# Two five-block feature buffers and filler block products in a four-layer graph kernel

## The chip, the cores and the metric

The kernel runs on one core of a Trainium2 chip, in 32-bit floats. The metric is the device time of one execution in microseconds (us). A profile of one further execution gives the span from its first to its last instruction and what each engine did: PE (TensorE, matrix products), DVE (VectorE), ACT (ScalarE), POOL (GpSimd), and SP (SyncE), which here only issues DMA transfers. PE's results land in PSUM, eight banks of 128 x 512 values.

## The reference

The input is 128 batches of 128 nodes x 512 features and one 128 x 128 matrix `adj`. Four layers follow each other, each added to its input and normalised over the features:

```python
x = _layernorm(x + _L0(x, adj, w0, bias0))        # adj @ x @ w0 + bias
x = _layernorm(x + _L1(x, w1, a, beta, adj))      # graph attention, elu
x = _layernorm(x + _L2(x, adj, adj, b2))          # reduces to relu(max_n(adj @ x) + b2)
x = _layernorm(x + _L3(x, w_qkv, w_proj, ..., adj))  # 8-head masked attention
```

Layer 3 makes q, k and v (512 x 1536 weights), scores of 8 heads of width 64, masks where `adj` is 0, a softmax, the product with v, a projection, and a normalisation with gamma and beta of its own, before the outer one.

## The kernel before, in words

**A batch** is one chain of steps (`batch`, L884). Layer 0: a product with `adj` (L281 for the first 12 batches, "direct"; later L300, whose result is transposed on DVE and regrouped by a trip through DRAM, x_d), a product with w0 (L273, four matmuls of 512 columns), then addition and normalisation. Layer 1: two logits per node (L920), an attention matrix made for two batches at a time (`attention1`, L577, which goes through DRAM twice, s_d and e_d), a product with it (L281), a product with w1 (L273), elu, normalisation. Layer 2: one product (L952), a maximum, normalisation. Then the features are transposed (L967) and sent to DRAM (`features`, L865), and the rows themselves are kept in DRAM too (`spill`, L870, `fetch`, L877).

**Groups.** Batches of one group share the work on q, k and v. There are 2 groups of two (FIRST), 28 of four (G) and 6 of two (PAIRS): 36. `gather` (L642) brings a group's features back, turned, as four blocks B11, B21, B12, B22, and POOL makes three further ones by four subtractions (L663): T3, T1 (in the place of B12), T2 and T4. The tile xT has seven blocks, and there is one such tile. `section` (L668), once each for q, k and v, makes the product with the weights as a 2 x 2 block product in Winograd's form: seven products instead of eight, each of 4 matmuls at L686 (256 columns in a group of four; 128 in a pair for q and k), with partial results copied by ACT (L721, L793) and added by DVE (L735). Three sections of seven products read xT, after which it is free.

**Attention** of layer 3: `tiled` and `score` (L803, L828) compute a group's scores (L834). Per batch DVE adds the mask (L984) and takes the maximum (L991), ACT takes eight exponentials (L1005), DVE multiplies by the reciprocal sums (L1012) and transposes (L1015); the probabilities go to DRAM (p_d, L1020) and come back regrouped (L1024), into the tile that held q and k. `attend` (L840) multiplies them with v (L855), two batches at a time, and `usual` (L1052) does the projection (L273), the sums and the output. q and k of a whole group lie in one tile qkT (two such tiles); v lies in one tile for each half of a group (four).

**What sets the order.** Nothing is scheduled by hand. `Plan` (L63) runs all chains against each other before the program is written. A step asks for an engine with its planned duration, and perhaps a buffer (`use`), and says with `late` how long after it its result is usable; a request is granted at the earliest time at which its engine, its inputs and its buffer are free, ties going by urgency and then by rank, the lower first. The granted order is the order of the instructions on each engine. The engines then run these in order, with semaphores where a result is needed, so the plan's durations decide only the order. A batch's rank is its number; block products have the group's first number plus SECTION (2) plus a part. The planned times of transfers are the `late` values of SP's steps. Buffers are counted in BUFS.

Small tiles (statistics, 128 x 1 values and the like) come from a pool that rotates through 12 buffers for each name.

Of the kernel before, what the change touches and what calls it, by code (L numbers as in the profile page):

```python
# [18 lines left out]
G = 4  # L19
FIRST = 2  # L20
PAIRS = 6
SOON = (0, 4, 0, 4, 10, 0)
# [3 lines left out]
RUN = 6  # L26
SECTION = 2
PACE = 0
# [11 lines left out]
    "ps": 8,  # L40
    "x": 12, "xr": 2, "yT": 4, "z": 1, "e": 1, "et": 1, "eT": 3, "t": 5, "xT": 1, "v": 4,
    "qkT": 2, "pt": 1,
}
LAST, AHEAD = 14, 4
DIRECT = 12
LATER = -0.1
LANDED = 4.0
# [3 lines left out]

B11, B21, B12, B22, T3, T2, T4 = range(7)
T1 = B12
BLOCKS = 7
A11, A12, A22, S1, S2, S3, S4 = range(7)
# [97 lines left out]
def gnn_stack_kernel(  # L153
# [22 lines left out]
    work = ctx.enter_context(tc.tile_pool(name="work", bufs=1))  # L176
    small = ctx.enter_context(tc.tile_pool(name="small", bufs=12))
    ps = ctx.enter_context(tc.tile_pool(name="ps", bufs=1, space=PSUM))
# [213 lines left out]
    def loads():  # L392
        yield use("SP", 0.4)
        nc.sync.dma_start(adj_sb, adj)
        landing(adj_in, P // 4)
        yield from load(0, "ACT", nc.scalar)
        w0_slot.append((yield use("SP", 0.0, "qkT")))
        w0_nat.append(
            buf(w0_slot[0], G, 2 * K, P).rearrange("p b c n -> p (b c n)")[:, : K * D].rearrange(
                "p (k o) -> p k o", k=K  # L400
            )
        )
        for k in range(K):
            yield use("SP", 0.4)
            nc.sync.dma_start(w0_nat[0][:, k, :], w0[k * P : (k + 1) * P])
            landing(w0_chunk[k], P)
        yield from load(1)
        yield use("SP", 0.4)
        nc.sync.dma_start(bias0_sb, rows(bias0, D))
        landing(bias0_in, P)  # L410
        for i in range(2, 4):
            yield from load(i)
        slot = yield use("SP", 1.0, "pt")
        matrix(w1_sb, w1)
        a_sb = buf(slot, H, P).rearrange("p (s k) f -> p s (k f)", s=2)
        nc.sync.dma_start(a_sb, rows(a, 2 * D).rearrange("p (s f) -> p s f", s=2))
        landing(w1_in, (K + 2) * P)
        plan.start(logit_rows(a_sb, slot), 0)
        for i in range(4, 8):
            yield from load(i)  # L420
        yield use("SP", 2.0)
        permuted(w0_sb, w0)
        landing(w0_in, K * P)
        yield use("SP", 1.0)
        nc.sync.dma_start(beta1_sb, rows(beta1, 1))
        nc.sync.dma_start(
            b2_sb, bass.AP(tensor=b2.tensor, offset=b2.offset, ap=[[1, P], [1, 1]])
        )
        landing(scalars_in, 2 * P)
        for i in range(8, 12):  # L430
            yield from load(i)
        yield use("SP", 2.5)
        permuted(wqkv_sb, w_qkv)
        matrix(wproj_sb, w_proj)
        for dst, src in ((bproj_sb, b_proj), (gamma_sb, gamma), (beta3_sb, beta3)):
            nc.sync.dma_start(dst, rows(src, D))
        landing(w3_in, (4 * K + 3) * P)
        plan.start(weight_sums(), 0)
        for i in range(12, NB):
            yield from load(i)  # L440
# [81 lines left out]
    class Group:  # L522


        def __init__(self, first, size):
            self.first, self.size, self.half = first, size, size // 2
            self.s = small.tile([P, G, 2], F32, name="s")
            self.logits = [Event(2) for _ in range(size // 2)]
            self.attention = [Event() for _ in range(size // 2)]
            self.summed, self.qk = Event(), Event(8)  # L530
            self.squared = [Event() for _ in range(size)]
            self.valued = [Event(2) for _ in range(2)]
            self.rows, self.attended, self.scored = ([Event() for _ in range(size)] for _ in range(3))
            self.heads, self.o, self.sc, self.scratch = {}, {}, {}, {}
            self.eT, self.xT, self.qkT, self.v, self.slot, self.left = {}, None, None, {}, {}, {}

# [18 lines left out]
    def group(i):  # L555

        g = group_of[i]
        if g not in groups:
# [6 lines left out]
            for s in range(3):  # L565
                plan.start(section(gr, s), rank + SECTION + (LATER if s == 2 else s / K))

# [9 lines left out]
    def attention1(gr, h):  # L577
# [14 lines left out]
        )  # L592
        bz = yield use("SP", 0.5, "z", late=2.2)
        z = buf(bz, 2, P)
# [36 lines left out]
        scratch = dram.tile([P, Q, 2 * S], F32, name="e_d")  # L631
        yield use("SP", 0.5, late=2.0)
        to_rows(et.rearrange("p c i s -> p c (i s)"), scratch)
# [8 lines left out]
    def gather(gr):  # L642

        n = gr.half * P
        for b in range(gr.size):
            yield gr.squared[b]
        landed = Event(gr.size)
        for b in range(gr.size):
# [8 lines left out]
            )  # L657
            done(landed, LANDED)
        yield landed
        yield w3_ready  # L660
        for out, a, b in ((T3, B22, B12), (T1, B12, B11), (T2, B22, T1), (T4, B21, T2)):
            yield use("POOL", 0.1 + 0.65 * gr.half)
            nc.gpsimd.tensor_tensor(  # L663
                gr.xT[:, out, :, :n], gr.xT[:, a, :, :n], gr.xT[:, b, :, :n], op=ALU.subtract
            )
        done(gr.summed)

    def section(gr, s):  # L668


        yield gr.summed
        half, n = gr.half, gr.half * P
# [3 lines left out]
        def multiply(p, w, block, first=False, final=False):  # L676
            w, t = weight(s, w), gr.xT[:, block]
            for j in range(half if s == 2 else 2):
                for k in range(2):
# [9 lines left out]
                    )  # L689
            gr.read("xT", 7 * 3)  # L690

        def into(t, i, j):

            if s == 2:
                shape = lambda x: x.rearrange("p (b f) -> p b f", b=half)
                return shape(t), gr.v[j][:, :half, i * D // 2 : (i + 1) * D // 2]
            dst = gr.qkT[:, j * half : (j + 1) * half, s * K + 2 * i : s * K + 2 * i + 2, :]
            return t.rearrange("p (c b n) -> p c b n", c=2, b=half), dst.rearrange(
                "p b c n -> p c b n"
            )  # L700
# [47 lines left out]

        extra = {2: ("v", "v")}.get(s, ())
        if s < 2 and gr.qkT is None:  # L750
            extra = ("qkT",)
        names = ("ps",) + extra
        got = yield use("PE", time, lambda: names[:1] if s < 2 and gr.qkT else names, late=0.2)
        if not isinstance(got[0], str):
            if s == 2:
                for j in range(2):
                    gr.slot["v", j] = got[1 + j]
                    gr.v[j] = buf(got[1 + j], 2, D)
            else:
                gr.slot["qkT"] = got[1]  # L760
                gr.qkT = buf(got[1], G, 2 * K, P)
            got = got[0]
# [9 lines left out]

        yield m1[0]
        yield use("PE", time, late=0.2)
        multiply(x, S2, T2)
        u2 = keep(x)

        by = yield use("PE", time, "ps", late=0.2)
        y = bank(by, D)[:, :wide]
        multiply(y, S3, T3, True)  # L780
        yield u2[0]
        yield use("PE", time, late=0.2)
        multiply(x, S1, T1)
# [13 lines left out]
        plan.start(last(bx), gr.first)  # L797
        yield c22
        yield use("PE", time, late=0.2)
        multiply(y, A22, T4, final=True)  # L800
# [27 lines left out]
    def score(gr, b, slots):  # L828

        p = [bank(slot, K, P) for slot in slots]  # L830
        for c in range(K):
            for j in range(2):
                rws = slice(j * HD, (j + 1) * HD)
                nc.tensor.matmul(  # L834
                    p[j][:, c, :], gr.qkT[rws, b, c, :], gr.qkT[rws, b, K + c, :],
                    start=True, stop=True,
# [11 lines left out]
    def attends(gr, bs, slots):  # L848
        for b, slot in zip(bs, slots):
# [3 lines left out]
            for c in range(K):  # L853
                for j in range(2):
# [4 lines left out]
                    )  # L859
            gr.read("qkT", gr.size)  # L860
            gr.o[b] = p, slot, v
# [8 lines left out]
    def spill(i, xb, biased, kept, spilled):  # L870
        yield biased
        yield use("SP", 0.5, late=2.5)
        nc.sync.dma_start(kept, xb)
# [3 lines left out]
    def fetch(i, kept, spilled, fetched):  # L877
        yield spilled
        x_slot[i] = yield use("SP", 0.5, "xr", late=3.0)
        xs[i] = buf(x_slot[i], D)  # L880
# [3 lines left out]
    def batch(i):  # L884
        yield loaded[i]
        gr, xb = group(i), xs[i]
        if group_of[i] >= RUN:
            yield groups[group_of[i] - RUN].summed
        paced = Event(0)
# [80 lines left out]
        biased = Event()  # L970
        plan.start(pool_add(xb, beta3_sb, biased), i)
        fetched = biased
# [7 lines left out]

        pr = gr.qkT[:, b]
        for j in range(2):
# [35 lines left out]
        scratch = dram.tile([P, Q, H * S], F32, name="p_d", bufs=8)  # L1018
        yield use("SP", 0.5, late=2.8)
        to_rows(pt.rearrange("p c h s -> p c (h s)"), scratch)  # L1020
        give(bt)
        yield use("SP", 0.5, late=4.0)
        prT = pr.rearrange("p h n -> p (h n)")
# [4 lines left out]
        yield gr.valued[j]  # L1028
        gr.heads[b] = gr.v[j][:, b % gr.half], prT
        done(gr.rows[b])  # L1030
        yield gr.attended[b]
        if i < NB - KEPT:
# [9 lines left out]
        yield from (last if i == NB - 1 else usual)(  # L1042
            i, oT, v, lambda: gr.read(("v", j), gr.half), fetched
        )
# [132 lines left out]
```

## Time and profile before

| | |
|---|---|
| median of 3 runs | 3250.27 us (3250.01 to 3250.68) |
| the profiled run | 3244.94 us, its span 3243.2 us |
| mean granted clock of PE | 0.985 of full |
| DMA | 429.53 MB, mean 132 GB/s |

Of the page, the busy shares of the engines and the 40 slices say which engine is at work all the time; the table of waits says for what an engine stood idle; the time line gives start and duration of merged instructions, with idle time before them and its cause in brackets. A 32-bit matmul appears as two passes, so a product of four matmuls is x8. Durations of matmuls overlap, so prices of PE are taken from start to start.

### The profile page before, as it was taken

The numbers are of one execution on the slowest core, as the hardware profiler recorded it, in microseconds if no ns is written. First come the engines' busy times: TensorE is split into PE (matmuls) and PEld (weight loads), VectorE is DVE, ScalarE is ACT, GpSimd is POOL, SyncE is SP. The second block draws the span as 40 slices with busy tenths as digits, with TensorE's granted clock in tenths as the row PEclk, the third lists the DMA queues.
The fourth block names the chain that finished last, engine by engine and source line by source line (L and its number), as shares of the span: only waits on it lengthen the run. The fifth ranks groups of instructions, "written<-read, shape, count | busy, mean of one in ns | idle before, by whom it ended". The sixth has DMA issues, their size and how long they took to land. (4 is left out here: it accounts for less than half of the span.)

```text
span 3243.2 us, 47028 instructions
## 1 busy us (share of the span) xinstructions
PE 3132.4 (97%) x14631; PEld 2083.0 (64%) x14631; DVE 2486.7 (77%) x5317; ACT 1778.4 (55%) x5182; POOL 1125.3 (35%) x1190
## 2 busy tenths in 40 slices
PE   8999999999998999999999999999999999999997
PEld 5675666666665756666576666666665666666675
DVE  7876777877778777778787778777787786876876
ACT  5554565565465545645645656555555554555553
POOL 5433224233335242332333324332433233332332
PEclk9999999999999999999999999999999999999999
DMA  4545336445336454354535545444545345442342
GB/s 167 143 140 127 94 126 179 139 113 161 92 115 185 122 133 120 134 163 120 156 97 164 146 121 156 138 106 129 163 127 157 102 131 154 140 138 82 113 121 85
DMA packets 766761, 429.53 MB, mean 132 GB/s; under 512 B 570032, under 2 KB 652336, under 8 KB 766512
## 3 DMA queue, kind: packets, MB, share of 16 engines
q1 hardware_dynamic: 766368, 426.26, 45.5%
q8 instruction: 118, 1.93, 0.2%
q14 instruction: 131, 1.07, 0.1%
q10 hardware_dynamic: 144, 0.26, 0.0%
HBM read 221.84 MB, written 204.54 MB: 131 GB/s over the span
## 5 line engine op out<-in xcount | busy, mean ns | idle before, releaser
L273 PE MATMUL ps<-w_sb,yT 128*128 128x512 f32 x1952 | 881.9, 599 | 21.1 <-DMA yT<-x_d 13.3
L216 POOL TENSOR_TENSOR rstd<-ve,neghalf 128x1 f32<-128x1 f32 x640 | 405.1, 637 | 1413.6 <-ACT ve L255 949.5
L273 PEld LDWEIGHTS ps<-w_sb,yT 128*128 128x128 f32 x1952 | 370.4, 192 | 426.6 <-issue 395.4
L686 PE MATMUL ps<-xT,wqkv_sb 128*128 128x256 f32 (+1 forms) x2304 | 484.1, 356 | 0.7 <-DVE qkT L735 0.7
L273 PE MATMUL ps<-wproj_sb,v 128*128 128x512 f32 x1016 | 456.1, 600 | 4.8 <-ACT v L1039 4.8
L686 PEld LDWEIGHTS ps<-xT,wqkv_sb 128*128 128x128 f32 x2304 | 402.9, 191 | 82.2 <-issue 35.6
L1005 ACT ACTIVATE qkT<-qkT,nmx 128x128 f32<-128x128 f32 x1008 | 392.8, 394 | 93.6 <-DVE nmx L991 68.1
L686 PE MATMUL ps<-xT,wsum_sb 128*128 128x256 f32 (+1 forms) x1728 | 370.6, 359 | 6.5 <-ACT t L721 4.8
L686 PEld LDWEIGHTS ps<-xT,wsum_sb 128*128 128x128 f32 x1728 | 303.3, 192 | 81.5 <-issue 35.6
L273 PEld LDWEIGHTS ps<-wproj_sb,v 128*128 128x128 f32 x1016 | 194.6, 193 | 229.3 <-issue 214.7
L721 ACT COPY t<-ps 128x512 f32<-128x512 f32 (+1 forms) x324 | 171.9, 534 | 245.2 <-PE ps L686 172.5
L663 POOL TENSOR_TENSOR xT<-xT 128x512 f32<-128x512 f32 (+1 forms) x144 | 176.1, 1223 | 291.2 <-DMA xT<-x_d 220.5
L250 ACT ACTIVATE t<-x,nm 128x512 f32<-128x512 f32 x263 | 188.7, 718 | 160.9 <-DVE nm L247 135.3
L686 PE MATMUL ps<-wqkv_sb,xT 128*128 128x256 f32 x1024 | 247.1, 382 | 0.0
L735 DVE TENSOR_TENSOR qkT<-ps,t 128x256 f32<-128x256 f32 (+1 forms) x324 | 178.6, 580 | 80.7 <-PE ps L686 42.9
L266 POOL TENSOR_TENSOR x<-x,beta_sb 128x512 f32<-128x512 f32 x128 | 173.3, 1356 | 160.9 <-DVE t L967 125.8
L920 DVE SCALAR_TENSOR_TENSOR t<-x,wa_rows 128x512 f32<-128x512 f32 x256 | 205.3, 804 | 27.6 <-ACT x L260 17.3
L686 PEld LDWEIGHTS ps<-wqkv_sb,xT 128*128 128x128 f32 x1024 | 193.0, 191 | 49.0 <-issue 22.6
L260 ACT ACTIVATE x<-x,nmr,rstd 128x512 f32<-128x512 f32 x263 | 214.4, 815 | 8.8
L266 POOL TENSOR_TENSOR xr<-xr,v 128x512 f32<-128x512 f32 x120 | 162.5, 1354 | 148.3 <-DMA xr<-x_s 65.4
L1015 DVE STREAM_TRANSPOSE pt<-qkT 128x1024 f32<-128x1024 f32 x128 | 158.4, 1237 | 65.9 <-DMA p_d<-pt 65.2
L259 ACT ACTIVATE nmr<-nm,rstd 128x1 f32<-128x1 f32 x383 | 111.7, 292 | 164.9 <-POOL rstd L216 164.0
(109 smaller groups left out, 4910.8 us busy)
## 6 DMA issues: line engine op xcount, KB each, us to landing
p_d<-pt SPq DMA_DIRECT2D x128, 512.0 KB
qkT<-p_d SPq DMA_DIRECT2D x128, 512.0 KB
x_d<-t SPq DMA_DIRECT2D x244, 256.0 KB
xT<-x_d SPq DMA_DIRECT2D x512, 64.0 KB
x<-in_x SPq DMA_DIRECT2D x127, 256.0 KB
x_s<-x SPq DMA_DIRECT2D x120, 256.0 KB
xr<-x_s SPq DMA_DIRECT2D x120, 256.0 KB
out<-xr SPq DMA_DIRECT2D x120, 256.0 KB
```

The costliest lines, as they stand in the source:

```text
L216: nc.gpsimd.tensor_tensor(rstd, ve, neghalf, op=ALU.pow)
L250: nc.scalar.activation(buf(b_sq, D), xb, AF.Square, bias=nm, accum_out=squares)
L260: nc.scalar.activation(xb, xb, AF.Identity, bias=nmr, scale=rstd)
L266: nc.gpsimd.tensor_tensor(dst, dst, other, op=ALU.add)
L273: nc.tensor.matmul(p, lhs(k), rhs(k), start=(k == 0), stop=(k == K - 1))
L663: nc.gpsimd.tensor_tensor(gr.xT[:, out, :, :n], gr.xT[:, a, :, :n], gr.xT[:, b, :, :n], op=ALU.subtract)
L686: nc.tensor.matmul(to, lhs, rhs, start=first and j == 0 and k == 0, stop=final and k == 1, skip_group_check=True,)
L721: nc.scalar.copy(held[1], p)
L735: nc.vector.tensor_tensor(c, a, b, op=ALU.add)
L920: nc.vector.scalar_tensor_tensor(buf(b_s, D), xb, 1.0, wa_rows[:, j, :], op0=ALU.mult, op1=ALU.mult, accum_out=gr.s[:, b, j : j + 1],)
L1005: nc.scalar.activation(pr[:, j, :], pr[:, j, :], AF.Exp, bias=nmx[:, j : j + 1], accum_out=sums[:, j : j + 1],)
L1015: nc.vector.transpose(pt.rearrange("p c h s -> p h c s"), pr.rearrange("p h (c r) -> p h c r", c=Q))
```

## The change

- Groups: FIRST 2 to 0 and PAIRS 6 to 2, so 31 groups of four and 2 of two: 33.
- xT has five blocks and there are two such tiles. T2 is written over B11 and T4 over B21, after all three sections have done their product with that block (`used`); a section waits for each T block by itself (`have`) and may begin when the features have landed and when the group before has all its scores.
- q and k have one tile for two batches, four in all, and are freed two by two.
- Block products have a rank ten higher (SECTION 12), those of v two more (LATER), so that they give way to everything nearby.
- Planned transfer times grow: z 2.2 to 3.4, e_d 2.0 to 2.6, the spill 2.5 to 3.5, the fetch 3.0 to 4.2, the write of p_d 2.8 to 4.0, its read-back 4.0 to 4.6.
- x tiles 12 to 10, small tiles 12 to 8; the subtractions are urgent; the addition of beta3 waits for the weights to have landed.

```diff
-FIRST = 2
-PAIRS = 6
+FIRST = 0
+PAIRS = 2
-SECTION = 2
+SECTION = 12
-    "x": 12, "xr": 2, ..., "xT": 1, "v": 4,
-    "qkT": 2, "pt": 1,
+    "x": 10, "xr": 2, ..., "xT": 2, "v": 4,
+    "qk": 4, "pt": 1,
-LATER = -0.1
+LATER = 2
-B11, B21, B12, B22, T3, T2, T4 = range(7)
-T1 = B12
-BLOCKS = 7
+B11, B21, B12, B22, T3 = range(5)
+T2, T4, T1 = B11, B21, B12
+BLOCKS = 5
-    small = ctx.enter_context(tc.tile_pool(name="small", bufs=12))
+    small = ctx.enter_context(tc.tile_pool(name="small", bufs=8))
...
 def attention1
-        bz = yield use("SP", 0.5, "z", late=2.2)
+        bz = yield use("SP", 0.5, "z", late=3.4)
-        yield use("SP", 0.5, late=2.0)
+        yield use("SP", 0.5, late=2.6)
...
 def gather
-        for out, a, b in ((T3, B22, B12), (T1, B12, B11), (T2, B22, T1), (T4, B21, T2)):
-            yield use("POOL", 0.1 + 0.65 * gr.half)
+        for out, a, b, when, t in (
+            (T3, B22, B12, None, T3), (T1, B12, B11, None, T1),
+            (B11, B22, T1, gr.used[B11], T2), (B21, B21, B11, gr.used[B21], T4),
+        ):
+            if when:
+                yield when
+            yield use("POOL", 0.1 + 0.65 * gr.half, urgent=True)
...
-        done(gr.summed)
+            done(gr.have[t], 0.1)
...
 def section
-        yield gr.summed
+        yield gr.landed
+        yield w3_ready
+        for event in before.scored if before else ():
+            yield event
...
+        yield gr.have[T2]
         yield use("PE", time, late=0.2)
         multiply(x, S2, T2)
...
 def attends
-            gr.read("qkT", gr.size)
+            gr.read(("qk", b // 2), 2)
...
 def spill / fetch
-        yield use("SP", 0.5, late=2.5)
+        yield use("SP", 0.5, late=3.5)
-        x_slot[i] = yield use("SP", 0.5, "xr", late=3.0)
+        x_slot[i] = yield use("SP", 0.5, "xr", late=4.2)
...
 def batch
-            yield groups[group_of[i] - RUN].summed
+            yield groups[group_of[i] - RUN].landed
-        plan.start(pool_add(xb, beta3_sb, biased), i)
+        plan.start(pool_add(xb, beta3_sb, biased, w3_in), i)
-        yield use("SP", 0.5, late=2.8)
+        yield use("SP", 0.5, late=4.0)
         to_rows(pt.rearrange("p c h s -> p c (h s)"), scratch)
-        yield use("SP", 0.5, late=4.0)
+        yield use("SP", 0.5, late=4.6)
```

More of the change, by code (lines that the diff above doesn't have):

```diff
@@ L40 @@
     "ps": 8,
-    "x": 12, "xr": 2, "yT": 4, "z": 1, "e": 1, "et": 1, "eT": 3, "t": 5, "xT": 1, "v": 4,
-    "qkT": 2, "pt": 1,
+    "x": 10, "xr": 2, "yT": 4, "z": 1, "e": 1, "et": 1, "eT": 3, "t": 5, "xT": 2, "v": 4,
+    "qk": 4, "pt": 1,
 }
@@ L396, in loads @@
         yield from load(0, "ACT", nc.scalar)
-        w0_slot.append((yield use("SP", 0.0, "qkT")))
+        w0_slot.append((yield use("SP", 0.0, "qk")))
         w0_nat.append(
-            buf(w0_slot[0], G, 2 * K, P).rearrange("p b c n -> p (b c n)")[:, : K * D].rearrange(
+            buf(w0_slot[0], 2, 2 * K, P).rearrange("p b c n -> p (b c n)").rearrange(
                 "p (k o) -> p k o", k=K
@@ L429, in loads @@
         landing(scalars_in, 2 * P)
-        for i in range(8, 12):
+        for i in range(8, BUFS["x"]):
             yield from load(i)
@@ L438, in loads @@
         plan.start(weight_sums(), 0)
-        for i in range(12, NB):
+        for i in range(BUFS["x"], NB):
             yield from load(i)
@@ L529, in __init__ @@
             self.attention = [Event() for _ in range(size // 2)]
-            self.summed, self.qk = Event(), Event(8)
+            self.landed, self.qk = Event(size), Event(8)
+            self.have = {t: Event() for t in (T1, T2, T3, T4)}
+            self.used = {t: Event(3) for t in (B11, B21)}
             self.squared = [Event() for _ in range(size)]
@@ L534, in __init__, with at, pair @@
             self.heads, self.o, self.sc, self.scratch = {}, {}, {}, {}
-            self.eT, self.xT, self.qkT, self.v, self.slot, self.left = {}, None, None, {}, {}, {}
+            self.eT, self.xT, self.slot, self.left = {}, None, {}, {}
+            self.qkT, self.v = [], []
+        def at(self, tiles, b):
+            return tiles[b // 2][:, b % 2]
+        def pair(self, tiles, j):
+            first = j * self.half
+            return tiles[first // 2][:, first % 2 : first % 2 + self.half]
         def read(self, name, of):
@@ L565, in group @@
             for s in range(3):
-                plan.start(section(gr, s), rank + SECTION + (LATER if s == 2 else s / K))
+                plan.start(
+                    section(gr, s, groups.get(g - 1)), rank + SECTION + (LATER if s == 2 else s / K)
+                )
             plan.start(tiled(gr, None, range(size)), rank)
@@ L646, in gather @@
             yield gr.squared[b]
-        landed = Event(gr.size)
         for b in range(gr.size):
@@ L657, in gather @@
             )
-            done(landed, LANDED)
-        yield landed
-        yield w3_ready
-        for out, a, b in ((T3, B22, B12), (T1, B12, B11), (T2, B22, T1), (T4, B21, T2)):
-            yield use("POOL", 0.1 + 0.65 * gr.half)
+            done(gr.landed, LANDED)
+        yield gr.landed
[6 more added lines that the diff above has]
+            yield use("POOL", 0.1 + 0.65 * gr.half, urgent=True)
             nc.gpsimd.tensor_tensor(
@@ L665, in gather, with section @@
             )
-        done(gr.summed)
-    def section(gr, s):
-        yield gr.summed
+            done(gr.have[t], 0.1)
+    def section(gr, s, before):
+        yield gr.landed
+        yield w3_ready
+        for event in before.scored if before else ():
+            yield event
         half, n = gr.half, gr.half * P
@@ L690, in multiply @@
             gr.read("xT", 7 * 3)
+            if first and block in gr.used:
+                done(gr.used[block], 0.1)
         def into(t, i, j):
@@ L695, in into @@
                 shape = lambda x: x.rearrange("p (b f) -> p b f", b=half)
-                return shape(t), gr.v[j][:, :half, i * D // 2 : (i + 1) * D // 2]
-            dst = gr.qkT[:, j * half : (j + 1) * half, s * K + 2 * i : s * K + 2 * i + 2, :]
+                return shape(t), gr.pair(gr.v, j)[:, :, i * D // 2 : (i + 1) * D // 2]
+            dst = gr.pair(gr.qkT, j)[:, :, s * K + 2 * i : s * K + 2 * i + 2, :]
             return t.rearrange("p (c b n) -> p c b n", c=2, b=half), dst.rearrange(
@@ L747, in release @@
             give(bank)
[L749 to L761, printed above, removed]
+        tiles, name = (gr.v, "v") if s == 2 else (gr.qkT, "qk")
+        got = yield use(
+            "PE", time, lambda: ("ps",) + (() if tiles else (name,) * (gr.size // 2)), late=0.2
+        )
+        if not tiles:
+            for m, slot in enumerate(got[1:]):
+                gr.slot[name, m] = slot
+                tiles.append(buf(slot, 2, D) if s == 2 else buf(slot, 2, 2 * K, P))
             got = got[0]
@@ L776, in section @@
         u2 = keep(x)
+        yield gr.have[T3]
         by = yield use("PE", time, "ps", late=0.2)
@@ L781, in section @@
         yield u2[0]
+        yield gr.have[T1]
         yield use("PE", time, late=0.2)
@@ L798, in section @@
         yield c22
+        yield gr.have[T4]
         yield use("PE", time, late=0.2)
@@ L830, in score @@
         p = [bank(slot, K, P) for slot in slots]
+        qk = gr.at(gr.qkT, b)
         for c in range(K):
@@ L834, in score @@
                 nc.tensor.matmul(
-                    p[j][:, c, :], gr.qkT[rws, b, c, :], gr.qkT[rws, b, K + c, :],
+                    p[j][:, c, :], qk[rws, c, :], qk[rws, K + c, :],
                     start=True, stop=True,
@@ L979, in batch @@
         sc, slots = gr.sc.pop(b)
-        pr = gr.qkT[:, b]
+        pr = gr.at(gr.qkT, b)
         for j in range(2):
@@ L1028, in batch @@
         yield gr.valued[j]
-        gr.heads[b] = gr.v[j][:, b % gr.half], prT
+        gr.heads[b] = gr.at(gr.v, b), prT
         done(gr.rows[b])
@@ L1042, in batch @@
         yield from (last if i == NB - 1 else usual)(
-            i, oT, v, lambda: gr.read(("v", j), gr.half), fetched
+            i, oT, v, lambda: gr.read(("v", b // 2), 2), fetched
         )
```

## The prediction

> **What bounds the kernel now.** I read the page's shares first, then TensorE's (PE's) busy time by stretch, then PE's waits, then the time line of one stall. In the page, the first line gives busy time, and the rows of digits the span in 40 slices:
>
> ```profile
> PE 3132.4 (97%) x14631; PEld 2083.0 (64%) x14631; DVE 2486.7 (77%) x5317; ACT 1778.4 (55%) x5182; POOL 1125.3 (35%) x1190
> ...
> PE   8999999999998999999999999999999999999997
> ```
>
> PE is the bound from end to end; nothing else is above 77%. A faster kernel has less PE work or less PE idle time, and the idle time is only 3243.2 - 3132.4 = 110.8 us. By stretch (width, then busy time and count of PE, PEld, DVE, ACT, POOL, granted clock, DMA share, GB/s):
>
> ```profile
> 0.00:150.00 150.00, 138.94 (x568) 84.47 (x569) 118.90 (x299) 82.24 (x197) 79.14 (x82) 0.98 0.49 159
> 150.00:2985.00 2835.00, 2760.87 (x12565) 1825.11 (x12564) 2173.71 (x4624) 1564.38 (x4562) 967.22 (x1016) 0.99 0.47 133
> 2985.00:3243.20 258.20, 232.57 (x1501) 173.43 (x1499) 194.13 (x396) 131.78 (x423) 78.96 (x92) 0.96 0.36 112
> ```
>
> Idle: 11.1 us at the start, 74.1 in the middle, 25.6 at the end. What PE waited for (total us, times, longest):
>
> ```profile
> PE ps L855 <- DMA qkT<-p_d: 41.2, 18, 4.3
> PE ps L273 <- DMA yT<-x_d: 13.3, 3, 6.1
> PE ps L686 <- ACT t L721: 11.9, 10, 2.3
> PE ps L281 <- DMA eT<-e_d: 7.9, 2, 5.2
> ```
>
> Over half is waiting for a round trip through DRAM, above all that of the probabilities (p_d) ahead of the attention products at L855. The time line of PE through the largest stall:
>
> ```profile
> 993.39 1.09 PE L855 MATMUL ps<-qkT,v 128*64 128x128 f32 x16
> 998.41 1.98 PE L855 MATMUL ps<-qkT,v 128*64 128x128 f32 x16 [3.92 <-DMA qkT<-p_d]
> ...
> 1012.99 3.60 PE L273 MATMUL ps<-w_sb,yT 128*128 128x512 f32 x8
> 1016.52 1.09 PE L855 MATMUL ps<-qkT,v 128*64 128x128 f32 x16
> 1019.74 1.09 PE L855 MATMUL ps<-qkT,v 128*64 128x128 f32 x16 [2.13 <-DMA qkT<-p_d]
> ```
>
> The same sixteen passes take 1.09 us before the stall and 1.98 after it: a stall is paid twice, as idle time and as a slowed clock. Two stretches around stalls show how much:
>
> ```profile
> 976.00:1022.00 46.00, 36.63 (x132) 17.61 (x132) 37.10 (x78) 22.53 (x65) 23.36 (x23) 0.93 0.87 228
> ...
> 2490.00:2520.00 30.00, 24.32 (x120) 15.88 (x119) 23.73 (x53) 10.41 (x22) 13.80 (x15) 0.89 0.77 246
> ```
>
> They hold 9.4 + 5.7 = 15.1 us of idle time, and lose 46 x 0.07 + 30 x 0.11 = 6.5 us of clock. Over seven such stretches (316-346, 976-1022, 1407-1430, 1596-1620, 2068-2084, 2490-2520, 2695-2720) it is 35.6 us idle and 18.5 us of lost clock, about half as much again. So the middle's 74 us cost some 74 + 37 = 111 us. The DMA share there is 0.77 and 0.87 against 0.47 on average: stalls sit where transfers bunch.
>
> **What the Trainium skill says.** "TensorE: Matmul & The Clock Gate", What's actually happening: the array falls to half rate after an idle window of about 3.4 us and needs a busy one to recover. The trace agrees (1.09 to 1.98 us), though here a gap of 3.92 us was enough and one of 2.13 was not. "DMA: Bandwidth & Descriptors", Latency and other measured facts: access to HBM takes 0.2 us on average and 2 us under heavy load. SyncE's (SP's) time line agrees in kind: from the issue of a p_d write to that of its read-back it is 2.75 us at 166.93 and 6.24 us at 979.44, where a burst of other issues also lies between. "Perfetto Trace Analysis", Optimization Strategy (of Identifying Performance Opportunities): the same gap, repeating, can mean too few buffers for the next tile. That fits: L686 has only 24.8 us of work between 955 and 1056, against 38.6 in the 95 us before, and that is where PE stood still longest.
>
> **The change, part by part** (lines are those of the kernel before; orders are those of the two built programs).
>
> *Groups.* 36 groups become 33: six pairs of batches become three groups of four. PE's time line prices it, start to start: two pair products, 3188.07 to 3189.86, are 1.79 us; one full product, 306.01 to 307.74, is 1.73. There are 7 x 2 such products (q and k) in each of three new groups: 42 x 0.06 = 2.5 us less. For v the pair's product (3189.86 to 3190.72, 0.86) is exactly half. The 39 evacuations fewer on ACT, 36 on DVE and 12 on POOL lie beside PE. Taken: -2.5.
>
> *Two feature buffers, block products as filler.* The 21 products of a group of four (about 36 us of PE) were spread over a median 71 us of PE work, where such a group's whole work is 3061/32 = 96 us (instruction counts times 0.86, 0.43 and 0.225 us per product of 512, 256 and 128 columns, and 0.94 a batch for scores and for attention, from time lines). In the new order the median is about 101, so that almost always some are at hand. Products that follow another into the same bank, with under 3.5 us of PE work between, go from 72 to 44, under 1.8 us from 13 to 4: of the 11.9 us behind ACT's L721 I leave 5.
>
> *Transfers given more time.* The planner's p_d write goes from 2.8 to 4.0 us and the read-back from 4.0 to 4.6: 1.8 more. No instruction is added; L855 comes later in PE's order. Between the end of a batch group's scores (L834) and its first attention pair the median PE work rises from 36.9 to 39.1 us, to the second pair from 46.8 to 50.3. Taking 2.2 us off each of the 15 p_d stalls in the middle (some 35 us) leaves about 12. Between L300 and its L273 the smallest distance rises from 4.3 to 11.1 us; the stall at 978 needed 8.6 (972.83 to 981.46), so of 13.3 I leave 1. The attention of layer 1 gets 1.2 + 0.6 more: of 7.9 I leave 4.
>
> *The rest.* Another 10 us of single waits (on ACT, DVE, POOL) stay. Left in the middle: 12 + 1 + 5 + 4 + 10 = 32 of 74 us: -42. The long stalls go first, and they brought the slow clock: of 37 I take 28 off. Sum -70.
>
> *x buffers, 12 to 10.* At the start two layer-0 batches (4 x 0.86 + 4 x 0.225 = 4.3 us each) no longer stand before the first L281; PE could idle up to 8.7 us, or nothing where the 5.67 us stall at 60.2 takes it up. Taken: +4.
>
> *Small tiles 12 to 8, the one wait added to beta3's addition.* Between nothing and one 0.64 us POOL operation per group, 21 us; taken as nothing, since a batch uses some five such tiles in the 24 us that PE gives it. The wait is for a weight landed long before.
>
> *In-place sums.* POOL's third and fourth subtraction now wait for all three sections' use of the block they overwrite. Behind them stand the rstd operations (L216), for which ACT waits. Four subtractions of 1.34 us per group stay; POOL is 35% busy. Between nothing and 10 us of waiting per group, of which a reserve covers 6.9 (the least PE work that the new order has between layer 1's L273 and L952), so up to 3.1 us on the path, 102 us in all; taken as nothing, since one PE product, 1.73 us, is the usual unit of lateness.
>
> *The end.* From the last scores' end (3201.7) to 3243.2 it is one batch's chain, with the same last products in both orders: nothing, though the group before gets 33 us instead of 25.
>
> Sum: -2.5 - 70 + 4 = -68.5 against the span of 3243.2, which is 1.7 us under its own run (3244.94); the median of the other three is 3250.27. 3250 - 69, rounded for the residues: 3180.
>
> **Rivals.** (1) All middle stalls go: 3250 - 2.5 - 111 = 3137. For it: every distance I looked at grew. Against: stalls hit groups with 40 us of distance (1557-1616) and spared one with 28 (2964), so chance in DVE's and SP's queues decides too. (2) Bursts move along: the same transfers, 429 MB, still bunch, and L855 waits as before; only the pair groups gain, and the start loses: 3245. (3) The slower one: POOL's in-order queue. A late block product holds the in-place subtraction, that holds the rstd operations behind it, and so the layernorms of other batches and their PE products. At 10 us of waiting in each of 33 groups, 3.1 beyond the reserve, it costs 102 us, half of that again in clock, against 69 won: 3250 - 69 + 153 = 3334. It decides from 1.4 us beyond the reserve (33 x 1.4 x 1.5 = 69), so from waits of 8.3 us. For it: ACT already waits 164 us for rstd. Against: POOL idles 65%. (4) The change doesn't do what it says: the planner's order keeps the distances; but the built order shows them moved.
>
> **The numbers.** Forecast (3155 to 3210) 0.63; rival 1 0.17; rival 2 0.09, about half of it below the mark; rival 3 0.09; rival 4 (no change) 0.02. A measurement of this kernel can tell about 0.2%, 6.5 us, from no change. Faster 0.63 + 0.17 + 0.05 = 0.85, same 0.06, slower 0.09. Range: from rival 1's 3138 to just under rival 2's, 3240, which leaves out rivals 3 and 4, most of 2 and the lower edge of 1: near 2 in 10.
>
> **What would show it.** Right: PE's middle idle time near 32 us, the p_d wait near 12 to 18 us in all, the clock back at 0.99 or more of full speed, PE busy near 3100 us (less slowed work). Wrong: a p_d wait still near 40; PE waiting for POOL's L663 or ACT's normalisations; over 20 us idle in the first 150 us.

## The result and the profile after

The changed kernel takes 3197.6 us (median; 3195.7 to 3199.1) against 3250.1 us: a ratio of 0.984 (95% interval 0.9823 to 0.9857), 52.6 us or 1.6% less. The forecast was 3180 us, the range 3138 to 3240. Times are medians of fast runs; one run of the last experiment, e12, took 11662 us, more than three times as long as its others, and is left out.

The page after, with the busy shares and the slices of the granted clock (only the last falls under 9 tenths):

```profile
span 3193.9 us, 46192 instructions
...
PE 3118.6 (98%) x14295; PEld 2063.0 (65%) x14295; DVE 2504.9 (78%) x5281; ACT 1768.6 (55%) x5143; POOL 1114.2 (35%) x1178
...
PEclk9999999999999999999999999999999999999998
```

PE's idle time went from 110.8 to 3193.9 - 3118.6 = 75.3 us, its busy time from 3132.4 to 3118.6. So 35.5 of the 49.3 us between the two spans are idle time, 13.8 busy time. By stretch, columns as before:

```profile
0.00:150.00 150.00, 135.73 (x474) 79.33 (x475) 115.00 (x280) 77.38 (x180) 79.46 (x81) 0.97 0.49 153
150.00:2985.00 2835.00, 2795.76 (x12710) 1844.76 (x12709) 2241.18 (x4719) 1591.59 (x4647) 975.62 (x1031) 1.00 0.48 136
```

Nearly all of it lies in the middle: 39.2 us idle instead of 74.1, with the clock from 0.99 to 1.00. The start is 3.2 us worse (14.3 instead of 11.1), the end 3.8 better (21.8 instead of 25.6). What PE waits for now:

```profile
PE ps L706 <- ACT t L743: 10.9, 7, 2.7
PE ps L273 <- ACT v L1061: 9.9, 5, 5.2
PE ps L281 <- DMA eT<-e_d: 9.4, 6, 5.2
PE ps L273 <- ACT yT L292: 9.3, 4, 3.3
PE ps L877 <- DMA qk<-p_d: 9.2, 6, 3.5
...
PE ps L273 <- DMA yT<-x_d: 0.5, 1, 0.5
```

L706, L743, L877 and L1061 are the former L686, L721, L855 and L1039. The wait for probabilities fell from 41.2 to 9.2 us, that for yT from 13.3 to 0.5. Nothing large took their place. Where block products lie has changed too: their busy time alone, in slices of 25 us of the same stretch of both runs (L686 before, L706 after; width, then busy time and count of PE and PEld, granted clock, DMA share, GB/s):

```profile
1550.00:1575.00 25.00, 1.89 (x8) 1.52 (x8) 1.00 0.20 62
1575.00:1600.00 25.00, 0.00 (x0) 0.00 (x0) 1.00 0.75 189
1600.00:1625.00 25.00, 0.00 (x0) 0.00 (x0) 0.93 0.91 254
1625.00:1650.00 25.00, 20.22 (x94) 18.01 (x95) 1.00 0.54 149
```

```profile
1550.00:1575.00 25.00, 4.65 (x21) 3.92 (x22) 1.00 0.09 34
1575.00:1600.00 25.00, 10.24 (x45) 8.08 (x43) 1.00 0.59 198
1600.00:1625.00 25.00, 12.52 (x56) 10.56 (x56) 1.00 0.64 158
1625.00:1650.00 25.00, 14.62 (x64) 11.99 (x64) 1.00 0.50 152
```

Before, 50 us pass without one block product, and two p_d stalls stand there, with the clock at 0.93 in the slice that holds them:

```profile
1600.33 1.09 PE L855 MATMUL ps<-qkT,v 128*64 128x128 f32 x16 [1.55 <-DMA qkT<-p_d]
...
1614.99 1.17 PE L855 MATMUL ps<-qkT,v 128*64 128x128 f32 x16 [3.75 <-DMA qkT<-p_d]
```

After, each slice has some block products. That goes along with the shorter waits; e5 below shows that it isn't enough by itself.

At the end, the time line of PE from the last scores on:

```profile
3146.23 2.06 PE L856 MATMUL ps<-qk 64*128 64x128 f32 x32
3150.35 1.69 PE L877 MATMUL ps<-qk,v 128*64 128x128 f32 x16 [2.07 <-DMA qk<-p_d]
3155.54 1.98 PE L877 MATMUL ps<-qk,v 128*64 128x128 f32 x16 [3.50 <-DMA qk<-p_d]
...
3172.57 6.38 PE L273 MATMUL ps<-wproj_sb,v 128*128 128x512 f32 x8 [5.24 <-ACT v L1061]
```

5.6 of the remaining 9.2 us of p_d wait are here, so the middle has 3.6. From the last scores' end to the end of the span it is 45.6 us, against 41.5.

### The profile page after: what moved, and what is told of

Same layout as the page of the kernel before. It is cut to its first block, busy times and chain, and to the rows that moved or that the text cites. A ratio compares the mean times of both kernels' runs of the same rounds, so it can differ in the third digit from the quotient of the medians.

```text
span 3193.9 us, 46192 instructions
## 1 busy us (share of the span) xinstructions
PE 3118.6 (98%) x14295; PEld 2063.0 (65%) x14295; DVE 2504.9 (78%) x5281; ACT 1768.6 (55%) x5143; POOL 1114.2 (35%) x1178
## 5 line engine op out<-in xcount | busy, mean ns | idle before, releaser
L273 PE MATMUL ps<-w_sb,yT 128*128 128x512 f32 x1952 | 874.9, 595 | 9.3 <-ACT yT L292 7.2
L273 PEld LDWEIGHTS ps<-w_sb,yT 128*128 128x128 f32 x1952 | 369.3, 191 | 410.6 <-issue 386.6
L706 PE MATMUL ps<-xT,wqkv_sb 128*128 128x256 f32 (+1 forms) x2112 | 474.0, 373 | 0.8 <-POOL xT L680 0.8
L273 PE MATMUL ps<-wproj_sb,v 128*128 128x512 f32 x1016 | 458.7, 603 | 14.6 <-ACT v L1061 9.9
L706 PEld LDWEIGHTS ps<-xT,wqkv_sb 128*128 128x128 f32 x2112 | 390.1, 190 | 79.0 <-issue 26.5
L1027 ACT ACTIVATE qk<-qk,nmx 128x128 f32<-128x128 f32 x1008 | 391.5, 391 | 25.8 <-DVE nmx L1013 25.5
L743 ACT COPY t<-ps 128x512 f32<-128x512 f32 (+1 forms) x297 | 168.5, 568 | 414.0 <-PE ps L706 230.7
L706 PE MATMUL ps<-xT,wsum_sb 128*128 128x256 f32 (+1 forms) x1584 | 357.4, 376 | 11.0 <-ACT t L743 10.9
L273 PEld LDWEIGHTS ps<-wproj_sb,v 128*128 128x128 f32 x1016 | 195.2, 193 | 251.1 <-issue 228.3
L706 PEld LDWEIGHTS ps<-xT,wsum_sb 128*128 128x128 f32 x1584 | 295.2, 192 | 76.5 <-issue 22.4
L942 DVE SCALAR_TENSOR_TENSOR t<-x,wa_rows 128x512 f32<-128x512 f32 x256 | 225.4, 881 | 56.6 <-ACT x L260 33.8
L706 PE MATMUL ps<-wqkv_sb,xT 128*128 128x256 f32 x1024 | 242.9, 380 | 0.0
L757 DVE TENSOR_TENSOR qk<-ps,t 128x256 f32<-128x256 f32 (+2 forms) x297 | 175.3, 620 | 84.5 <-PE ps L706 37.9
L706 PEld LDWEIGHTS ps<-wqkv_sb,xT 128*128 128x128 f32 x1024 | 192.2, 190 | 54.5 <-issue 25.2
L266 POOL TENSOR_TENSOR x<-x,bias_sb 128x512 f32<-128x512 f32 x128 | 176.1, 1386 | 118.0 <-PE ps L300 107.1
L1037 DVE STREAM_TRANSPOSE pt<-qk 128x1024 f32<-128x1024 f32 x128 | 158.4, 1238 | 42.0 <-DMA p_d<-pt 41.5
```

The source lines that it names most:

```text
L266: nc.gpsimd.tensor_tensor(dst, dst, other, op=ALU.add)
L273: nc.tensor.matmul(p, lhs(k), rhs(k), start=(k == 0), stop=(k == K - 1))
L706: nc.tensor.matmul(to, lhs, rhs, start=first and j == 0 and k == 0, stop=final and k == 1, skip_group_check=True,)
L743: nc.scalar.copy(held[1], p)
L757: nc.vector.tensor_tensor(c, a, b, op=ALU.add)
L942: nc.vector.scalar_tensor_tensor(buf(b_s, D), xb, 1.0, wa_rows[:, j, :], op0=ALU.mult, op1=ALU.mult, accum_out=gr.s[:, b, j : j + 1],)
```

## The experiments

Three explanations were open. Theory A: the planned transfer times were too short, and giving them more is the gain. Theory B: PE lacked work at those places, and spreading block products is the gain. Theory C: they need each other, and the second buffer is what allows both. All ratios are to the kernel before, with 95% intervals.

**Planned times alone, on the kernel before (e1).**

```diff
 # kernel before
-z 2.2, e_d 2.0, spill 2.5, fetch 3.0, p_d write 2.8, read-back 4.0
+z 3.4, e_d 2.6, spill 3.5, fetch 4.2, p_d write 4.0, read-back 4.6
```

> The kernel before with the six planned transfer times of the changed kernel and nothing else. Theory A (margin: the round trips were planned too short, and L855 stood too early in PE's order): most of the gain comes with this edit alone; the p_d wait falls from 41 us to under 15 us, the time to 3205-3220 us. Theory B (filler: PE had nothing to do at those places, since one feature buffer and the low rank bunched the block products): the waits move to other causes or into the plan's own idle time, and the time stays at 3240-3255 us.

Measured: 3237.2 us, ratio 0.9965 (0.9954 to 0.9975). PE's waits:

```profile
PE ps L273 <- DMA yT<-x_d: 24.3, 9, 6.0
PE ps L855 <- DMA qkT<-p_d: 23.1, 11, 5.1
PE ps L952 <- ACT x L260: 11.9, 3, 10.7
PE ps L300 <- DMA x<-in_x: 8.9, 1, 8.9
```

The p_d wait is nearly halved, but other waits grow: yT from 13.3 to 24.3, the loads of x from nothing to 8.9. That is under a quarter of the change's gain. Theory A alone falls.

**The changed kernel with the old times (e2)**, the same six numbers the other way.

> The changed kernel with the six planned transfer times of before. Theory A: the p_d wait comes back to 30 us or more and the time to 3225-3245 us. Theory B: block products fill the places, the time stays at 3195-3210 us.

Measured: 3267.4 us, ratio 1.006 (1.0044 to 1.0077), slower than the kernel before and above both forecasts.

```profile
PE ps L877 <- DMA qk<-p_d: 42.4, 18, 4.7
PE ps L273 <- ACT yT L292: 12.7, 5, 3.3
PE ps L877 <- DVE rs L1033: 10.3, 1, 10.3
```

The p_d wait is all back, although buffers and ranks are those of the changed kernel. Theory B alone falls too: a plan that believes the transfers are short puts L877 too early, although the filler is there (no slice of this run either is without a block product). The six numbers are worth 70 us in the changed kernel, 12 us in the old one.

**Old ranks in the changed kernel (e3).**

```diff
-SECTION = 12
+SECTION = 2
-LATER = 2
+LATER = -0.1
```

> The changed kernel with the ranks of before for block products (SECTION 2, LATER -0.1), two feature buffers kept. Theory B in its form 'rank': block products bunch again as before, PE idles between bunches, 3230-3250 us. Theory A: the margin is in the transfer times, 3195-3210 us.

Measured: 3384.9 us, ratio 1.0424 (1.0408 to 1.044).

```profile
PE ps L300 <- DMA x<-in_x: 66.2, 11, 13.5
PE ps L974 <- ACT x L260: 64.5, 16, 7.1
PE ps L273 <- DMA yT<-x_d: 27.4, 12, 6.5
```

Far above what any theory gave. PE waits for x tiles to be loaded, and for normalisations. The block products are bunched: three slices in a row without one.

```profile
1550.00:1575.00 25.00, 6.05 (x26) 4.48 (x24) 1.00 0.21 69
1575.00:1600.00 25.00, 0.00 (x0) 0.00 (x0) 1.00 0.12 43
1600.00:1625.00 25.00, 0.00 (x0) 0.00 (x0) 1.00 0.62 206
1625.00:1650.00 25.00, 0.00 (x0) 0.00 (x0) 1.00 0.60 183
```

Of the 113 slices of 25 us from 150 to 2975 us, 28 are without a block product; in the kernel before it is 6, in the changed kernel none.

**Old groups in the changed kernel (e4)**: FIRST 2 and PAIRS 6.

> The changed kernel with the groups of before (2 pairs at the start, 6 at the end, 36 groups). By the price of the two product forms alone it costs 2.5 us more PE work: 3200 us. If the pairs at the start fed PE earlier, or those at the end shortened the last chain, it is at or under 3197 us; if groups of four matter for the spread of block products, over 3206 us.

Measured: 3206.4 us, ratio 0.9872 (0.9858 to 0.9887). That is 8.8 us over the changed kernel, where the product forms alone give 2.5. PE's busy time is 4.8 us more (3123.4), its idle time 6.1 us more (81.4). At most, the groups are a small part of the gain.

**One buffer in the changed kernel (e5)**: "xT" 2 to 1.

> The changed kernel with one five-block feature buffer in place of two; ranks, times, groups and all else kept. Theory C (margin and filler need each other: with longer planned transfers L855 stands later only if block products are at hand to fill the time, and they can be spread over a group's whole period only if the next group's features have a buffer of their own): block products of one group have to end before the next ones' features come in, 3225-3300 us. Theory D (rank and planned times do it, the second buffer is idle reserve): 3195-3210 us.

Measured: 3471.5 us, ratio 1.0701 (1.0683 to 1.0719).

```profile
PE ps L877 <- DMA qk<-p_d: 102.8, 36, 7.2
PE ps L706 <- DMA xT<-x_d: 26.8, 7, 7.5
PE ps L273 <- DMA yT<-x_d: 26.2, 12, 5.3
```

PE now waits for features (26.8 us), as theory C says, and more than in the kernel before for everything that goes through DRAM. Theory D falls, by more than theory C had expected. But the reason that theory C gave is not what the trace shows: the block products are not bunched. As in the changed kernel, none of the 113 slices from 150 to 2975 us is without one. So the new ranks spread the products here with one buffer as with two, and a spread alone gains nothing. How the missing buffer leads to the p_d wait of 102.8 us was not followed and stays open.

**New ranks in the kernel before (e6), and with the new times too (e7)**; both keep one seven-block buffer, twelve x tiles and the old groups.

> The kernel before with the new ranks (SECTION 12, LATER 2), one seven-block buffer and the old planned times. Theory C: products held back keep the single buffer longer, and the p_d wait stays at 35 us or more: 3245-3300 us. Theory D: rank alone gains, 3215-3240 us.

> The kernel before with new ranks and new planned times, still one seven-block buffer, its groups and 12 x tiles. Theory C: without the second buffer the pair gains no more than the planned times alone did, 3230-3300 us. Theory D: it comes near the changed kernel, 3197-3215 us.

Measured: 3340.2 us (1.0294; 1.0277 to 1.0311) and 3423.0 us (1.0549; 1.053 to 1.0567). PE's waits in e6:

```profile
PE ps L855 <- DMA qkT<-p_d: 73.3, 29, 19.8
PE ps L686 <- DMA xT<-x_d: 21.0, 5, 4.8
```

Theory D falls. Theory C has the direction right, and in e6 the p_d wait, but both times lie above its ranges. Without the second buffer, the ranks lose 3%, and ranks and times together 5%.

**A control (e8)**: one planned time of the changed kernel, the read-back of p_d, 4.6 to 4.7.

> Control: the changed kernel with one planned time nudged, the read-back of p_d 4.6 to 4.7 us. No theory gives it a cost; it only reshuffles the planned order. It shows how far two equally good orders lie apart: within 8 us of 3197 us if differences of 10 us between my runs can be read as effects of the edits, 15 us or more away if they cannot.

Measured: 3197.9 us, ratio 0.9859 (0.9844 to 0.9873), so the same time by an order of its own. One such pair doesn't bound the scatter of orders; I read differences of 70 us and more as effects, and leave those under some 20 us open.

**The space for the second buffer (e9)**: ten x tiles in the kernel before.

```diff
-    "x": 12,
+    "x": 10,
-        for i in range(8, 12):
+        for i in range(8, 10):
-        for i in range(12, NB):
+        for i in range(10, NB):
```

> The kernel before with ten x tiles in place of twelve and nothing else: the cost of the space that the second feature buffer takes. My prediction gave it 4 us, at the start: 3245-3258 us. If x tiles feed PE through the whole run (the changed kernel with its old ranks waited 66 us for x loads), 3280 us or more, and the second buffer's own worth in the changed kernel is larger than its net gain.

Measured: 3370.1 us, ratio 1.0367 (1.0346 to 1.0389): 119 us for two tiles.

```profile
PE ps L855 <- DMA qkT<-p_d: 59.4, 24, 16.9
PE ps L686 <- ACT t L721: 36.5, 18, 6.8
PE ps L281 <- DMA eT<-e_d: 27.3, 10, 4.0
PE ps L273 <- DMA yT<-x_d: 23.8, 4, 7.5
```

Each of these four waits grows, while only 12.0 us are waits for x itself. It fits that PE, with fewer batches under way, has less other work to put in front of a result that is on its way; no run tries this apart.

**Eleven x tiles in the changed kernel (e10)**, with small tiles 8 to 6 to make room, **and more reserve (e11)**: MARGIN 1.0 to 1.5.

> The changed kernel with eleven x tiles, the space taken from small tiles (8 to 6). If x tiles are short in it too: 3180-3192 us. If block products fill whatever an x tile would have fed: within 6 us of 3197 us.

> The changed kernel with half a microsecond more planned reserve ahead of each product of PE (MARGIN 1.0 to 1.5). Theory C: margin against PE's lateness is paid for by filler, so the remaining waits (ACT's copies, about 20 us in all, and the rest) shrink: 3178-3192 us. If the filler is used up by now, the plan has to leave PE idle: 3200 us or more.

Measured: 3219.0 us (0.9903; 0.9884 to 0.9923) and 3210.7 us (0.9876; 0.9857 to 0.9895). Neither is better than the changed kernel, and e10 fits neither of its two forecasts. In e11 the wait for ACT's copies of v fell from 9.9 to 4.3 us and that at L706 from 10.9 to 5.6, but the p_d wait rose from 9.2 to 32.6, 16.5 of it in one stall. e10 changes two things, and which of them cost 21 us wasn't tried alone; what grew most is the p_d wait (20.6) and one stall of 10.6 us for yT. Both may be no more than orders drawn anew.

**The fourth corner (e12)**: one buffer and the old ranks in the changed kernel.

> The changed kernel with one five-block feature buffer and the old ranks (SECTION 2, LATER -0.1); planned times, groups and ten x tiles of the changed kernel. It is the fourth corner beside two buffers with old ranks (3385 us), one buffer with new ranks (3472 us) and both new (3198 us). Theory C (each of the two is worth nothing without the other): 3370-3410 us, so the second buffer gains under 25 us with old ranks while it gains 274 us with new ones. Rival (a second buffer helps by itself, by letting features come in early): 3435 us or more.

Measured: 3363.3 us, ratio 1.0347 (1.0327 to 1.0368), just under theory C's range. With this the four corners, all with ten x tiles, 33 groups and the new times, are:

| | old ranks | new ranks |
|---|---|---|
| one buffer | 3363 us | 3472 us |
| two buffers | 3385 us | 3198 us |

Against one buffer with old ranks, the second buffer alone loses 22 us, about what I leave open between two orders, and the new ranks alone lose 108; both together gain 166. Theory C is shown in its main point: the second buffer and the filler ranks are worth something only together (274 us for the buffer under new ranks, nothing under old ones), and most of the longer planned times' worth comes only on top of them (70 us instead of 12). Why they need each other is shown in part: old ranks leave gaps without block products with one buffer too (24 of the 113 slices of e12), and one buffer makes PE wait for features.

Both corners with old ranks lie near the 3370 us of e9, the kernel before with ten x tiles. Seen from there the rest of the change wins 172 us, against 53 us seen from the kernel before: it first makes up for the two x tiles. Other parts of the change (q and k in tiles for two batches, urgent subtractions, the start of a section after the scores of the group before, fewer small tiles) are in all four corners, and no run takes one of them back alone.

## Why the prediction was right, point by point

The direction and the main step were right: the waits behind round trips through DRAM went, because longer planned times and block products at hand moved their users back in PE's order. Of 69 us foreseen 53 came. That the sum fits is in part luck: it adds the parts as if each had a worth of its own, and the experiments show terms of 70 to 274 us that hang on one another.

- **p_d wait.** I left 12 us in the middle; 3.6 stayed. For yT I left 1 us; 0.5 stayed in all. For eT I left 4; of its 9.4 us 5.2 are one stall at the start, so 4.2.
- **ACT's copies at L743.** I left 5 us, since fewer products follow closely in one bank; 10.9 stayed against 11.9. The counts of close pairs fell, but they didn't show which pairs stall. This term was mis-sized.
- **Single waits.** I left 10 us; what remains of the middle, 39.2 - 3.6 - 0.5 - 4.2 - 10.9, is 20.
- **Clock.** I took 28 us off for it. Over the whole run the loss is 1 - 0.985 of 3243.2, 48.6 us, before, and 1 - 0.992 of 3193.9, 25.6 us, after: 23 less. But part of the slow clock falls into PE's idle time, where it costs nothing, and the prediction counted that too. Half rate was granted for 94.7 us before and 50.0 after; PE was busy for 72.4 and 37.9 us of these, and at half rate it loses half of that: 36.2 and 19.0 us, 17 less. In the middle alone it is 28.9 before, where the prediction had 37, and 7.8 after: 21 less instead of 28. With the 2.5 us of the groups PE's busy time should have fallen by some 20 us; it fell by 13.8. Part of the difference may be the scores: L834 was busy for 125.0 us, L856 is for 130.6. The rest wasn't located.
- **Groups.** 2.5 us by the product forms; e4 puts the whole edit at 8.8, within what orders may scatter.
- **x buffers.** I took +4 at the start; it is 3.2 of idle time, and 3.2 more of slow clock, since PE works at half rate for 10.2 us there instead of 3.8. But the reading that ten tiles cost something at the start alone was wrong for the kernel that I read it from: there they cost 119 us (e9). The changed kernel doesn't show such a cost. That block products now do there what the two more batches did is a reading: an eleventh tile gained nothing (e10), but took small tiles away. If it holds, the sum over parts hid two large terms of opposite sign, and +4 was right by luck.
- **In-place sums (the slower rival).** POOL does wait for the products, in lines of the waits after:

```profile
POOL xT L680 <- PE ps L706: 138.4, 40, 20.6
...
ACT nmr L259 <- POOL rstd L216: 124.2, 148, 2.9
```

  but ACT's wait for the rstd operations, which stand in the same queue, fell from 164.0 to 124.2 us, its longest from 7.2 to 2.9, and PE's own wait for POOL's sums is 0.8 us. Taking it as nothing was right, though not because the waits are short: the longest, 20.6 us, is twice what this rival allowed.
- **The end.** Taken as nothing, it is 4.1 us longer; the wait for ACT ahead of the last L273, 5.24 us, was 1.95 before.
- **The other rivals.** That all middle stalls go didn't come: 39 us of idle time stay. That bursts move along didn't either, though e2 shows it in a form: with the old times the stalls are back. That the change does nothing is ruled out by the interval.

## What to carry to other kernels

Where the bound engine waits for round trips that a static order placed too early, look for two things together: honest latencies in the plan, and work without a deadline to put in the time they open. In this kernel such work also needed a second buffer: held back with one, it lost 3 to 7% (e5, e6, e7). Measure such edits together and at the corners: here, made alone on the kernel before, the planned times gained 0.4% and the ranks lost 3%, and the smaller number of x tiles that pays for the buffer lost 4%. When space moves from one buffer to another, price what it did where it was: here two x tiles were worth 119 us.

## What was not expected of the hardware

The slow clock needs no gap as long as the 3.92 us of the prediction. In the kernel before, PE stood idle for 2.10 us ahead of L273 at 820.12 and for 2.13 us ahead of L855 at 1019.74. The granted clock (the third figure from the right) in the stretches that follow:

```profile
820.60:824.00 3.40, 3.40 (x5) 1.35 (x4) 3.23 (x9) 1.55 (x4) 1.31 (x2) 0.50 0.00 0
```

```profile
1020.80:1024.60 3.80, 3.80 (x10) 1.78 (x10) 1.48 (x5) 0.93 (x2) 3.29 (x4) 1.00 0.98 340
```

Half rate after the one, full rate after the other: the length of a gap alone doesn't decide. In both profiles each stretch at half rate lasts 3.41 us or two or three times as long, but for the one that the end of the span cuts off.

The scores of a group's four batches come less often in one piece: in 17 of 31 groups of four after, in 26 of 28 before, by the time line. The source view of the score products gives what ended PE's (and its weight loads') idle time ahead of them, after:

```profile
  issue: 16.2, 27
  DVE qk L1006: 6.1, 10
```

L1006 is DVE's mask addition, which frees the banks of the first scores; its counterpart L984 isn't among these lines before. That it is banks held by unfinished sections that force this wait is argued from the order, not tried.
